# Tying layer-norm statistics to an earlier block's conv1, and moving taps and spectra stores to ScalarE's queue

## The chip, the cores and the metric

The kernel runs on one core of a Trainium2 chip. The metric is the device time of one execution in microseconds. The kernel before was run three times: 1967.88, 1967.87 and 1965.79 us, median 1967.87 us. One more execution was taken with the hardware profiler.

The engines are named as in the profile: PE is TensorE's matmul, PEld its weight load, DVE VectorE, ACT ScalarE, POOL GpSimd and SP SyncE. SPq and ACTq are the places in SP's and ScalarE's instruction streams where DMAs are issued.

## What is computed

Two graph layers run over x of shape 128 graphs × 128 nodes × 256 features, float32. In each layer the input is layer-normalised and rectified, and the layer's output is added to x. The first layer is a convolution branch and a message branch joined by gates like those of a GRU; the second is a sum of five small graph convolutions over fixed subsets of the nodes. What matters here is the convolution branch of the first layer:

```python
h = jnp.maximum(_layernorm(x, axis=-1), 0.0)          # into layer 0
xc = jnp.transpose(x, (0, 2, 1))                      # x is h here
h = _bn(_conv1d(xc, conv1_w, 0), bn1_g, bn1_b, bn1_m, bn1_v)
h = jax.nn.relu(h)
h = _bn(_conv1d(h, conv2_w, 8), bn2_g, bn2_b, bn2_m, bn2_v)
x_conv = jnp.transpose(jax.nn.relu(h + xc), (0, 2, 1))
```

`conv1` is a product with a 256 × 256 matrix. `conv2` has 17 taps along the nodes, and the kernel computes it in a frequency domain.

## The kernel before, in words

A block is four graphs (`BB`, line 18), so there are 32 blocks; a half is 64 graphs (`HG`), or 16 blocks. The kernel has a front part and a gates part. The front part ends at about 530 us, and the change lies in it.

**Weight spectra** (`weight_spectra`, line 153). The taps of conv2 come in eight pieces. For each, `taps_load` (line 147) reads 1024 KB into one of two `w2` buffers, TensorE transforms it in four groups of four PSUM banks (line 160), and the sixteen banks are copied into `sp`, of which there are two buffers: three of each four copies by ScalarE (line 168) and the fourth by VectorE (line 166). The finished `sp`, 2560 KB, is stored to the DRAM tensor `vd` (line 170). SP issues both the loads and the stores.

**Heads** (lines 173 to 272). For block i, `head_load` (line 175) reads 512 KB of x into a buffer `ln`. `head_stats` (line 179) makes mean and variance on VectorE (lines 184, 185, 187) and the power -1/2 on GpSimd (line 189). `head_norm` (line 192) normalises in place on VectorE. `head_turn` (line 198) transposes on TensorE (line 205), rectifies on ScalarE into `ht` (line 206) and stores `ht` to DRAM (line 207). `head_conv1` (line 210) multiplies on TensorE (line 219), adds the shift on VectorE (line 222) and rectifies on ScalarE (line 223) into `h1`. `head_spectra` (line 226) transforms `h1` on TensorE (line 234) into `X`, with copies on VectorE (line 240) and ScalarE (line 242).

The loop in `heads` (line 255) is a software pipeline over i: load block i + `ahead`, conv1 of block i, turn of block i + 1, norm of block i + 2, spectra of block i − 1, statistics of block i + 3. In the first half `ahead` is 5, and twice per block `between()` puts two groups of a weight spectrum in. In the second half `ahead` is 3 and `between()` does nothing.

**Spectral stage** (`spectral`, line 274). For each of 40 frequencies p, the weight spectra `v` are loaded by SP (line 284, two DMAs of 512 KB per pair of frequencies, three `v` buffers). VectorE makes `s` (line 297), GpSimd makes `vs` (line 299, three buffers), TensorE makes three products (lines 302 and 307), ScalarE copies the first to `k1` (line 304) and VectorE adds (line 308); ScalarE issues the stores to `yd` (line 311). Eight frequencies before its end, `near_end` calls `heads_begin` (line 244) for the next half, which loads three blocks of x on SP and starts their statistics.

**Gate weights** (`gate_weights`, line 321). After the first spectral stage in program order stand the loads of `wih` and `whh` (lines 383 and 384) and twelve GpSimd operations (lines 326 to 329), which write the three tiles `sw`. They are used only in the gates part.

**What sets the order.** The program is written as a stream of operations on tiles. A list scheduler orders each engine's instructions by its own estimate of when they are ready, within the dependences between tiles; it therefore may put an operation ahead of others that stand before it in the text. [...] The trace shows such moves: the load of `fw` (line 382) is issued at 36.70 us, amid the first half's heads.

Of the kernel before, what the change touches and what calls it, by code (L numbers as in the profile page):

```python
# [21 lines left out]
NP_ = LW // 2  # L22
WCH = 64
# [51 lines left out]
def gnn_kernel(ctx: ExitStack, tc: tile.TileContext, io, out0: bass.AP, out1: bass.AP):  # L75
    nc = tc.nc
# [15 lines left out]
    def bank():  # L92
        return psum.tile([P, 512], F32, tag="bank", name="bank")
# [50 lines left out]
    vd = dram.tile([C, D // WCH, P, LW, WCH], F32, tag="vd", name="vd")  # L144
    yd = [dram.tile([HG, 2, LW, D], F32, tag=f"yd{h}", name=f"yd{h}") for h in range(NH)]

    def taps_load(pool, c, q, split=1):
        w2 = pool.tile([P, WCH // 4, P], F32, tag="w2", name="w2", bufs=2)
        for t in range(0, WCH // 4, WCH // 4 // split):
            nc.sync.dma_start(w2[:, t:t + WCH // 4 // split], io["w2t"][:, c, q, t:t + WCH // 4 // split])  # L150
        return w2

    def weight_spectra(pool, c, q, w2):

        sp = pool.tile([P, LW, WCH], F32, tag="sp", name="sp", bufs=2)
        for t in range(WCH // 16):
            ps = [bank() for _ in range(4)]
            for j in range(4):
                for r in range(4):
                    nc.tensor.matmul(ps[r][:, j * LW:(j + 1) * LW], w2[32 * r:32 * r + KW, 4 * t + j, :],  # L160
                                     gt[32 * r:32 * r + KW, :], start=True, stop=True)
            for r in range(4):
                o0 = t * 16 + 4 * r
                dst, s = sp[:, :, o0:o0 + 4], ps[r][:, :4 * LW].rearrange("p (j d) -> p d j", j=4)
                if r == 3:
                    nc.vector.tensor_copy(dst, s)
                else:
                    nc.scalar.copy(dst, s)
            yield
        nc.sync.dma_start(vd[c, q], sp)  # L170


    xs, stats, hcs, h1s = {}, {}, {}, {}

    def head_load(pool, ahead, i, queue):
        xs[i] = pool.tile([P, BB, D], F32, tag="ln", name="ln", bufs=ahead)
        queue.dma_start(xs[i], x[i * BB:(i + 1) * BB].rearrange("b n d -> n b d"))

    def head_stats(wk, i):

        mv = wk.tile([P, BB, 2], F32, tag="mv", name="mv", bufs=3)
        st = wk.tile([P, BB, 6], F32, tag="st", name="st", bufs=2)
        for b in range(BB):
            nc.vector.bn_stats(st[:, b, :], xs[i][:, b, :])
            nc.vector.bn_aggr(mv[:, b, :], st[:, b, :])
        ve = wk.tile([P, BB], F32, tag="ve", name="ve", bufs=2)
        nc.vector.tensor_scalar(ve, mv[:, :, 1], EPS, None, op0=ALU.add)  # L187
        rs = wk.tile([P, BB], F32, tag="rs", name="rs", bufs=3)
        nc.gpsimd.tensor_tensor(rs, ve, mhalf, op=ALU.pow)  # L189
        stats[i] = mv, rs  # L190
# [53 lines left out]
    def heads_begin(wk, xk, ahead, h):  # L244

        i = h * NBH
        for k in range(1 if h == 0 else 0, ahead):
            head_load(xk, ahead, i + k, nc.sync)
        for k in range(1 if h == 0 else 0, 3):
            head_stats(wk, i + k)  # L250
            if k < 2:
                head_norm(i + k)
        head_turn(wk, i)

    def heads(wk, xk, ahead, X, h, between):

        i0, i1 = h * NBH, (h + 1) * NBH
        for i in range(i0, i1 + 1):
            if i + ahead < i1:
                head_load(xk, ahead, i + ahead, nc.sync)  # L260
            if i < i1:
                head_conv1(wk, i)
            between()
            if i + 1 < i1:
                head_turn(wk, i + 1)
            if i + 2 < i1:
                head_norm(i + 2)
            between()
            if i > i0:
                head_spectra(X, i - 1)  # L270
            if i + 3 < i1:
                head_stats(wk, i + 3)

    def spectral(bp, X, h, near_end):

        for p0 in range(0, NP_, 4):
            if p0 == NP_ - 8:
                near_end()
            ys = bp.tile([P, 4, 2, D], F32, tag="ys", name="ys", bufs=2)
            for p in range(p0, p0 + 4):  # L280
                if p % 2 == 0:
                    v = bp.tile([P, C, D // WCH, 4, WCH], F32, tag="v", name="v", bufs=3)
                    for c in range(C):
                        nc.sync.dma_start(v[:, c], vd[c, :, :, 2 * p:2 * p + 4, :].rearrange("q i d o -> i q d o"))
                vr, vi = v[:, :, :, 2 * (p % 2), :], v[:, :, :, 2 * (p % 2) + 1, :]
                a, d = X[:, :, p, 0, :], X[:, :, p, 1, :]
                y = ys[:, p - p0]
                ps = bank()
                if p == 0:
                    for k, (u, w) in enumerate(((a, vr), (d, vi))):  # L290
                        for c in range(C):
                            nc.tensor.matmul(ps[:, k * D:(k + 1) * D], u[:, c], w[:, c], start=c == 0, stop=c == C - 1)
                    nc.scalar.copy(y.rearrange("p k o -> p (k o)"), ps)
                    continue

                s = bp.tile([P, C, P], F32, tag="s", name="s", bufs=2)
                nc.vector.scalar_tensor_tensor(s, a, -2.0, d, op0=ALU.mult, op1=ALU.subtract)  # L297
                vs = bp.tile([P, C, D // WCH, WCH], F32, tag="vs", name="vs", bufs=3)
                nc.gpsimd.tensor_tensor(vs, vr, vi, op=ALU.add)  # L299
                p1 = bank()  # L300
                for c in range(C):
                    nc.tensor.matmul(p1[:, :D], a[:, c], vs[:, c], start=c == 0, stop=c == C - 1)  # L302
                k1 = bp.tile([P, D], F32, tag="k1", name="k1", bufs=2)
                nc.scalar.copy(k1, p1[:, :D])  # L304
                for k, (u, w) in enumerate(((s, vi), (d, vr))):
                    for c in range(C):
                        nc.tensor.matmul(ps[:, k * D:(k + 1) * D], u[:, c], w[:, c], start=c == 0, stop=c == C - 1)  # L307
                nc.vector.tensor_tensor(y, ps.rearrange("p (k o) -> p k o", k=2),  # L308
                                        k1[:, None, :].to_broadcast([P, 2, D]), op=ALU.add)
            for w in range(2):  # L310
                nc.scalar.dma_start(yd[h][:, w, 2 * p0:2 * p0 + 8, :].rearrange("g d o -> g (d o)"),
                                    ys[w * HG:(w + 1) * HG].rearrange("p a k o -> p (a k o)"))
# [18 lines left out]
    with front as es:  # L331
# [3 lines left out]
        with ExitStack() as ws:  # L335

            xk = ws.enter_context(tc.tile_pool(name="xk", bufs=1, side="right"))
            wp = ws.enter_context(tc.tile_pool(name="wp", bufs=1))
            ahead = 5
            todo = [(c, q) for c in range(C) for q in range(D // WCH)]  # L340
            head_load(xk, ahead, 0, nc.scalar)
            nc.sync.dma_start(gt, io["gt"])
            taps = [taps_load(wp, *todo[k], split=1 if k else 4) for k in range(2)]
            head_stats(hk, 0)
            head_norm(0)
            spectra = []

            def some_spectra(k=1):
                for _ in range(k):
                    if not spectra and todo:  # L350
                        spectra.append(weight_spectra(wp, *todo.pop(0), taps.pop(0)))
                    if spectra and next(spectra[0], STOP) is STOP:
                        spectra.pop(0)
                        if len(todo) > 1:
                            taps.append(taps_load(wp, *todo[1]))
                        some_spectra()

            some_spectra(3)
            constants()
            heads_begin(hk, xk, ahead, 0)  # L360
            some_spectra(3)
            heads(hk, xk, ahead, X, 0, lambda: some_spectra(2))
            while spectra or todo:
                some_spectra()
        gw = ctx.enter_context(tc.tile_pool(name="gw", bufs=1, side="right", reuse_waits="tile"))
        xk = es.enter_context(tc.tile_pool(name="xk1", bufs=1, reuse_waits="tile"))
# [6 lines left out]
        sw = [gw.tile([P, 3, 3, P], F32, name=f"sw{k}") for k in range(3)]  # L373
# [13 lines left out]
    wk = ctx.enter_context(tc.tile_pool(name="wk", bufs=1, reuse_waits="tile"))  # L387
# [716 lines left out]
```

## Time and profile before

| what | us |
|---|---|
| median of three runs | 1967.87 |
| profiled execution, its own time | 1969.54 |
| profiled execution, span from first to last instruction | 1967.8 |
| TensorE matmul busy | 1911.4 |
| VectorE busy | 1288.8 |
| ScalarE busy | 711.4 |
| GpSimd busy | 610.3 |

The mean granted clock of TensorE is 0.984 of full speed. Busy times of different engines overlap. A row of the profile for a group of instructions gives line, engine, operation, what is written from what is read, the count, the busy time and the mean of one; a bracket after an instruction in order of time gives how long its engine had been idle and what ended that.

The largest transfers of the front part, by the page's list of DMA issues, are:

| transfer | issued by | times | KB each |
|---|---|---|---|
| v from vd | SP | 80 | 512 |
| vd from sp | SP | 8 | 2560 |
| ht to DRAM | ScalarE | 32 | 512 |
| x | SP (one by ScalarE) | 31 + 1 | 512 |
| taps | SP | 7 of 1024, 4 of 256 | |

### The profile page before, as it was taken

The numbers are of one execution on the slowest core, as the hardware profiler recorded it, in microseconds if no ns is written. First come the engines' busy times: TensorE is split into PE (matmuls) and PEld (weight loads), VectorE is DVE, ScalarE is ACT, GpSimd is POOL, SyncE is SP. The second block draws the span as 40 slices with busy tenths as digits, with TensorE's granted clock in tenths as the row PEclk, the third lists the DMA queues.
The fourth block names the chain that finished last, engine by engine and source line by source line (L and its number), as shares of the span: only waits on it lengthen the run. The fifth ranks groups of instructions, "written<-read, shape, count | busy, mean of one in ns | idle before, by whom it ended". The sixth has DMA issues, their size and how long they took to land.

```text
span 1967.8 us, 29919 instructions
## 1 busy us (share of the span) xinstructions
PE 1911.4 (97%) x10418; PEld 1664.8 (85%) x10418; DVE 1288.8 (65%) x3255; ACT 711.4 (36%) x1438; POOL 610.3 (31%) x681
## 2 busy tenths in 40 slices
PE   8889997999999999999999999999999999999998
PEld 7778886998878888888878888888878888888887
DVE  6556445855468777777756677777756677777643
ACT  4444112531133433433434433333434433333334
POOL 1011641115423344344322143343322143343300
PEclk9899998999999999999999999999999999999999
DMA  8885795439863323323423533322423533322135
GB/s 312 324 290 179 229 314 183 164 123 293 282 197 84 90 67 92 89 69 79 121 59 98 129 107 83 95 71 70 123 71 94 130 94 94 84 71 56 51 90 148
DMA packets 248853, 265.76 MB, mean 135 GB/s; under 512 B 106850, under 2 KB 223927, under 8 KB 244223
## 3 DMA queue, kind: packets, MB, share of 16 engines
q1 hardware_dynamic: 240367, 225.58, 39.6%
q10 hardware_dynamic: 8336, 38.28, 5.1%
q8 instruction: 83, 1.36, 0.3%
q14 instruction: 67, 0.55, 0.1%
HBM read 178.66 MB, written 85.14 MB: 134 GB/s over the span
## 4 chain that ended last, share of the span: by engine, by line
PE 89%; DMA 5%; DVE 3%; POOL 1%; issue 1%; ACT 1%; SPq 0%; POOLq 0%; DVEq 0%; ACTq 0%
PE bank L565 44%; PE bank L307 6%; PE bank L471 6%; PE bank L884 5%; PE bank L824 5%; PE bank L219 5%; PE bank L302 3%; PE bank L517 3%; PE bank L453 3%; DMA ln<-in_x_dram 3%; PE bank L234 2%; PE bank L456 1%; PE bank L504 1%; PE bank L803 1%; PE bank L735 1%; PE bank L205 1%
## 5 line engine op out<-in xcount | busy, mean ns | idle before, releaser
L565 PE MATMUL bank<-t,sw 128*128 128x256 f32 x1152 | 290.7, 379 | 0.0
L578 POOL TENSOR_TENSOR u<-u,m 128x256 f32<-128x256 f32 x128 | 93.0, 726 | 595.2 <-ACT m L576 546.3
L565 PEld LDWEIGHTS bank<-t,sw 128*128 128x128 f32 x1152 | 215.6, 190 | 29.7 <-issue 2.3
L565 PE MATMUL bank<-t,wih 128*128 128x256 f32 x768 | 197.2, 379 | 0.0
L565 PEld LDWEIGHTS bank<-t,wih 128*128 128x128 f32 x768 | 143.4, 190 | 19.3 <-DVE u L583 0.5
L219 PE MATMUL bank<-wc,ht 128*128 128x256 f32 x512 | 130.0, 411 | 13.9 <-ACT ht L206 13.2
L299 POOL TENSOR_TENSOR vs<-v 128x512 f32<-128x512 f32 x78 | 101.1, 1315 | 130.1 <-DMA v<-vd 73.7
L219 PEld LDWEIGHTS bank<-wc,ht 128*128 128x128 f32 x512 | 103.7, 207 | 32.1 <-ACT ht L206 16.3
L471 PE MATMUL bank<-wms,ht 128*128 128x259 f32 x512 | 122.3, 381 | 0.0
L884 PE MATMUL bank<-w,hh 128*125 128x256 f32 (+9 forms) x480 | 113.6, 380 | 1.0 <-DVE hh L829 1.0
L565 PE MATMUL bank<-t,whh 128*128 128x256 f32 x384 | 114.4, 379 | 0.0
L565 PE MATMUL bank<-xn,wih 128*128 128x256 f32 x384 | 114.2, 379 | 0.0
L565 PE MATMUL bank<-xc,wih 128*128 128x256 f32 x384 | 114.2, 379 | 0.0
L297 DVE SCALAR_TENSOR_TENSOR s<-X 128x256 f32<-128x256 f32 x78 | 52.5, 675 | 91.9 <-PE bank L307 91.7
L565 PE MATMUL bank<-ht,whh 128*128 128x256 f32 x384 | 110.2, 381 | 0.0
L471 PEld LDWEIGHTS bank<-wms,ht 128*128 128x128 f32 x512 | 97.2, 190 | 14.6
L824 PE MATMUL bank<-ax,w 128*128 128x500 f32 (+8 forms) x416 | 107.0, 396 | 0.2 <-DMA w<-in_w_dram 0.2
L583 DVE TENSOR_TENSOR u<-bank,u 128x256 f32<-128x256 f32 x128 | 53.7, 419 | 74.0 <-PE bank L565 74.0
L189 POOL TENSOR_TENSOR rs<-ve,mhalf 128x4 f32<-128x4 f32 x32 | 32.3, 1009 | 225.2 <-DVE ve L187 225.2
L884 PEld LDWEIGHTS bank<-w,hh 128*125 128x125 f32 (+9 forms) x480 | 84.3, 178 | 19.3 <-DVE hh L829 1.6
L475 ACT ACTIVATE msg<-msg 128x512 f32<-128x512 f32 x64 | 40.3, 630 | 162.6 <-DVE msg L472 160.2
L304 ACT COPY k<-bank 128x256 f32<-128x256 f32 x78 | 28.9, 372 | 178.6 <-DVE ys L308 69.8
(190 smaller groups left out, 4307.1 us busy)
## 6 DMA issues: line engine op xcount, KB each, us to landing
v<-vd SPq DMA_DIRECT2D x80, 512.0 KB
vd<-sp SPq DMA_DIRECT2D x8, 2560.0 KB
yd<-ys ACTq DMA_DIRECT2D x40, 512.0 KB
w<-in_w_dram SPq DMA_DIRECT2D x40, 512.0 KB
htd<-ht ACTq DMA_DIRECT2D x32, 512.0 KB
ht<-htd SPq DMA_DIRECT2D x32, 512.0 KB
ym<-yd SPq DMA_DIRECT2D x32, 512.0 KB
xt<-in_xT_dram SPq DMA_DIRECT2D x32, 512.0 KB
```

Source lines behind the costliest of these rows:

```text
L219: nc.tensor.matmul(pv[:, bb, :], ht[:, c, b * N:(b + 1) * N], wc1[:, c, :], start=c == 0, stop=c == C - 1)
L299: nc.gpsimd.tensor_tensor(vs, vr, vi, op=ALU.add)
L302: nc.tensor.matmul(p1[:, :D], a[:, c], vs[:, c], start=c == 0, stop=c == C - 1)
L307: nc.tensor.matmul(ps[:, k * D:(k + 1) * D], u[:, c], w[:, c], start=c == 0, stop=c == C - 1)
L453: nc.tensor.matmul(ps[:, b * N:(b + 1) * N], ym[:, b, o * P:(o + 1) * P], idm, start=b == 0, stop=False)
L471: nc.tensor.matmul(ps[:, :D + 3], ht[:, c, b * N:(b + 1) * N], wms[:, c, :], start=c == 0, stop=c == C - 1)
L517: nc.tensor.matmul(ps[:, b * N:(b + 1) * N], msg[:, b, c * P:(c + 1) * P], e[:, b, :], start=True, stop=True)
L565: nc.tensor.matmul(ps, w, d, start=n == 0, stop=n == len(pairs) - 1)
L578: nc.gpsimd.tensor_tensor(got["u4"], got["u2"], got["m5"], op=ALU.add)
L583: nc.vector.tensor_tensor(got["u3"], ps, got["u2"], op=ALU.add)
L824: nc.tensor.matmul(pv[:, q - q0, :], w1s[k5 + g][:, c, q * P:(q + 1) * P], xv[:, c], start=c == 0, stop=c == C - 1)
L884: nc.tensor.matmul(ps[:n1, :D], hh[:, q, at:at + n1], w2s[k5 + g][:, q, :], start=q == 0, stop=q == HID // P - 1)
```

## The change

There are four edits. First, `head_stats` takes an optional tile `behind`: if it is given, ScalarE copies one column per graph of it into the statistics buffer `st` before VectorE's statistics overwrite that place. In `heads` the tile is `h1s[i]`, the output of conv1 of block i, for the statistics of block i + 3. Secondly, ScalarE issues the spectra stores and all taps loads but the first two; of the last four copies of a spectrum, the one that VectorE made is made by ScalarE. Thirdly, the first three x loads of the second half are issued by ScalarE in place of SP. Fourthly, at frequency 20 of the first half, GpSimd copies one column of `k1` into each tile `sw`, in a place that the gate weights' first operation writes.

```diff
-    def taps_load(pool, c, q, split=1):
+    def taps_load(pool, c, q, queue, split=1):
         w2 = pool.tile([P, WCH // 4, P], F32, tag="w2", name="w2", bufs=2)
         for t in range(0, WCH // 4, WCH // 4 // split):
-            nc.sync.dma_start(w2[:, t:t + WCH // 4 // split], io["w2t"][:, c, q, t:t + WCH // 4 // split])
+            queue.dma_start(w2[:, t:t + WCH // 4 // split], io["w2t"][:, c, q, t:t + WCH // 4 // split])
...
-                if r == 3:
+                if r == 3 and t < WCH // 16 - 1:
                     nc.vector.tensor_copy(dst, s)
                 else:
                     nc.scalar.copy(dst, s)
             yield
-        nc.sync.dma_start(vd[c, q], sp)
+        nc.scalar.dma_start(vd[c, q], sp)
...
-    def head_stats(wk, i):
+    def head_stats(wk, i, behind=None):
...
+        if behind is not None:
+            nc.scalar.copy(st[:, :, 0], behind[:, :, 0])
         for b in range(BB):
             nc.vector.bn_stats(st[:, b, :], xs[i][:, b, :])
...
-            head_load(xk, ahead, i + k, nc.sync)
+            head_load(xk, ahead, i + k, nc.scalar if h else nc.sync)
...
-                head_stats(wk, i + 3)
+                head_stats(wk, i + 3, h1s[i])
...
+                if h == 0 and p == NP_ // 2:
+
+                    for t in sw:
+                        nc.gpsimd.tensor_copy(t[:, 0, 1, 0:1], k1[:, 0:1])
...
-            taps = [taps_load(wp, *todo[k], split=1 if k else 4) for k in range(2)]
+            taps = [taps_load(wp, *todo[k], nc.sync, split=1 if k else 4) for k in range(2)]
...
-                            taps.append(taps_load(wp, *todo[1]))
+                            taps.append(taps_load(wp, *todo[1], nc.scalar))
```

## The prediction

> **What bounds the kernel now.** I read the page first, then the busy time by stretches of the span, then the waits of TensorE and VectorE inside the stretches that are not full, and last the order of time around the longest waits.
>
> ```profile
> PE 1911.4 (97%) x10418; PEld 1664.8 (85%) x10418; DVE 1288.8 (65%) x3255; ACT 711.4 (36%) x1438; POOL 610.3 (31%) x681
> ...
> PEclk9899998999999999999999999999999999999999
> ```
>
> TensorE is the bound: 1911.4 of 1967.8 us, so idle time can give back at most 56.4 us. A second reserve is the granted clock, which falls below 1 only in the first third of the span. By stretches (length, then busy time of PE, PEld, DVE, ACT and POOL, granted clock, DMA share, GB/s):
>
> ```profile
> 22.20:125.00 102.80, 89.88 (x1106) 78.51 (x1102) 57.30 (x191) 48.98 (x134) 10.06 (x10) 0.87 0.82 305
> 125.00:196.30 71.30, 64.81 (x369) 57.69 (x369) 46.50 (x151) 27.74 (x74) 12.49 (x12) 0.95 0.67 233
> 196.30:215.00 18.70, 15.90 (x67) 13.20 (x66) 7.64 (x11) 2.50 (x7) 16.53 (x16) 0.91 0.51 169
> 295.00:340.00 45.00, 32.83 (x151) 27.36 (x150) 24.03 (x63) 10.45 (x26) 9.31 (x8) 0.85 0.57 181
> 345.00:425.00 80.00, 80.00 (x495) 74.50 (x494) 58.78 (x198) 40.15 (x102) 9.47 (x10) 1.00 0.39 139
> ```
>
> The first row is the heads with the weight spectra, the second the rest of the first half's heads, the third the start of its spectral stage, the fourth the end of that stage and the first heads of the second half, the fifth those heads in full run: TensorE never idle, VectorE idle for 21.2 us. Ceiling of each row, idle plus busy time times (1 − clock): 12.9 + 11.7 = 24.6; 6.5 + 3.2 = 9.7; 2.8 + 1.4 = 4.2; 12.2 + 4.9 = 17.1. Together 55.6 us. The waits between 22 and 125 us (total, times, longest), TensorE's:
>
> ```profile
> PE bank L160 <- DVE sp L166: 10.1, 3, 4.1
> PE bank L234 <- DVE sp L166: 2.1, 4, 0.6
> ```
>
> and one of VectorE's:
>
> ```profile
> DVE st L184 <- DMA ln<-in_x_dram: 9.5, 4, 4.4
> ```
>
> In order of time, one of the two four-microsecond waits:
>
> ```profile
> 47.21 0.33 SPq L170 DMA_DIRECT2D vd<-sp  x1
> ...
> 47.64 0.38 SPq L177 DMA_DIRECT2D ln<-in_x_dram  x1
> ...
> 62.09 0.75 DVE L184 BATCH_NORM_STATS2 st<-ln 128x6 f32<-128x256 f32 x2 [4.31 <-DMA ln<-in_x_dram]
> ...
> 63.76 0.46 DVE L166 COPY sp<-bank 128x320 f32<-128x320 f32 x1
> ...
> 64.28 2.01 PE L160 MATMUL bank<-gt,w 17*128 17x80 f32 x32 [4.02 <-DVE sp L166]
> ```
>
> The load of block 7 is issued 0.43 us after a 2560 KB spectra store on the same queue and is used 14.4 us later. VectorE has already reached that block's statistics, though conv1 has only done blocks 0 to 2 by then; it stands there, and the eviction that TensorE needs stands behind it. The same happens at 105.5 to 109.6 us, and twice in the second half:
>
> ```profile
> 284.38 0.44 SPq L177 DMA_DIRECT2D ln<-in_x_dram  x1
> ...
> 295.34 0.75 DVE L184 BATCH_NORM_STATS2 st<-ln 128x6 f32<-128x256 f32 x2 [6.38 <-DMA ln<-in_x_dram]
> ...
> 297.97 1.48 PE L307 MATMUL bank<-v,s 128*128 128x256 f32 x4 [2.57 <-issue]
> ...
> 315.81 28.95 SPq L177 DMA_DIRECT2D ln<-in_x_dram  x4
> ...
> 324.11 0.75 DVE L184 BATCH_NORM_STATS2 st<-ln 128x6 f32<-128x256 f32 x2 [8.47 <-DMA ln<-in_x_dram]
> ...
> 330.38 6.61 PE L219 MATMUL bank<-wc,ht 128*128 128x256 f32 x16 [6.72 <-ACT ht L206]
> ```
>
> The last row also shows the clock: conv1 of a block takes 6.61 us here and 3.45 us in the chain's undisturbed blocks. At 194.7 us GpSimd starts the twelve gate-weight operations as soon as their load lands, and TensorE's next product waits behind them:
>
> ```profile
> 194.73 1.96 POOL L326 TENSOR_TENSOR sw<-wih 128x384 f32<-128x384 f32 x2 [17.10 <-DMA wih<-in_wih_dram]
> ...
> 208.82 1.14 PE L302 MATMUL bank<-vs,X 128*128 128x256 f32 x4 [2.79 <-POOL vs L299]
> ```
>
> [...] after the 4.02 us wait, 65 to 70 us has a granted clock of 0.51. [...]
>
> **The change, part by part.** The sums are made against the profiled execution, 1969.5 us (span 1967.8), which is 1.7 us above the median of the runs, 1967.9.
>
> *Statistics behind conv1.* Adds 26 ScalarE copies of 128x4 (13 in each half). The nearest row is the 128x5 exponential, 0.23 us: 26 × 0.23 = 6 us of ScalarE, which is busy 49.0 of 102.8 and 40.2 of 80 us, so it hides. VectorE's statistics of block i+3 now wait for the ReLU of conv1 of block i; behind them stand evictions, norms and spectra copies, for which TensorE waits. With x loaded five ahead in the first half, block 7's statistics come after conv1 of block 4, past 84 us, while x was there at 62. The waits at 60 and 105 us go: 4.02 + 4.08 us idle, and the clock with them (65–70: 5.0 × 0.49; 60–65: 0.98 × 0.20; 110–115: 5.0 × 0.42; 105–110: 0.92 × 0.26) = 5.0. Together −13. What is late next is the sp slot: a period moves 2560 + 1024 + 512 + 512 KB = 4.7 MB; the store issues lie 14.7 us apart on average (22.15 to 125.04 in seven periods), 11.4 in the shortest. At the 440 to 455 GB/s of the fullest 5 us stretches the data alone need 10.5 us, and TensorE's work (two times 2.03 for the spectrum, 3.45 + 0.9 + 2.17 for the head) 10.6. A mean of 14.7 − 13/7 = 12.8 us is inside both. Bounds: −5, if stores become late, to −20.
>
> In the second half, block 19's statistics can't stand before conv1 of block 16 at 311 us, so the wait at 295 goes whole: 2.57 + 1.83 idle and about 1.0 of clock = 5.4. For block 20 they follow conv1 of block 17 (ends 320.5), its x lands at 324, and the evictions and the ReLU of block 18's turn are ahead of them: of 1.06 + 6.72 idle and 3 of clock I count half. With 5.4 that is about −10; bounds −5 and −15. In the full run the tie costs nothing while it stays below VectorE's spare 21.2 / 12.3 = 1.7 us per block.
>
> *Taps and spectra stores on ScalarE.* Six tap loads (0.33 us to issue) and eight stores (0.33) leave SP for ScalarE: 14 × 0.33 = 4.6 us. The eight copies that go from VectorE to ScalarE are 8 × 0.44 = 3.5 us there and 3.9 less on VectorE; a store then waits for nothing younger than ScalarE's own copy. SP's waits for them (58.7 for taps, 45.6 for the spectra) leave x's path. A tap load waits for the last product of its spectrum, which ScalarE's next copies need anyway. Behind a store on the ACT row now stand taps and the ht stores; ht is needed again only after 500 us. I take 0 on the path; bounds −3 and +5 if issuing stretches (SP's x loads reached 1.42 us each).
>
> *x of the second half by ScalarE.* Three issues, previously at 145.8 us on SP and 4.3 us long; their statistics and two norms (about 7 us of VectorE) ran amid the heads there, with 6.5 us of TensorE idle. Less crowding on SP and earlier x for blocks 13 to 15: −3, bounds 0 and −7.
>
> *Gate weights held to the middle of the first spectral stage.* Adds three one-column copies on GpSimd, between 0.1 (a memset of 128x4) and 1.0 us (the power) each. It removes the block of 12 operations ahead of L299 at 207 us: −3 of the ceiling 4.2. The twelve (about 1.07 us each, 12.9 in all) then go into a stage in which a frequency takes TensorE 2.6 us and GpSimd 1.3; if they sit in the gaps they cost nothing, in a row 12.9 less three vs buffers (7.8) = 5, plus clock. I take +3.
>
> Sum: −13 − 10 − 3 − 3 + 3 = −26 on the path: 1943.5 for the profiled kind of execution, 1942 against the median.
>
> **Rivals.** *Transfers hold the front.* The 31.5 MB between 22 and 125 us already move at a DMA share of 0.82; stores and taps land later beside x, sp slots come late and the −13 vanishes. For it: the share of 0.8 to 1.1 in most 5 us stretches; against: the 11.4 us period. Then 1968 − 13 = 1955. *All goes*: the tie and the free queue take most of the 55.6: about 1922. *It doesn't do what it says*: the new order has waits of the same size elsewhere, within 3 us of before. *VectorE becomes the bound through the tie (slower).* Per block it is busy 58.78 / 12.3 = 4.8 us of 6.5. If the order puts statistics at once behind conv1's eviction, each block adds the ReLU (0.63), the copy and crossings (0.4), and the wait for GpSimd's power (1.2) before a norm right behind: with the X and conv1 waits that remain (about 0.9), 7.9 us. It decides from 1.7 us of added wait per block; 1.4 us over in each of 23 heads outside the DMA-bound part is 32 us, and clock on top, against some 16 gained: 1984. Against it: one iteration lies between statistics and norm in program order.
>
> **How the numbers follow.** Likeliest, 1942 (its own range 1930 to 1953): 0.52. Transfers hold the front, 1955: 0.22. All goes, 1922: 0.08. No effect: 0.05. VectorE bound, 1984: 0.13. A difference of 0.2%, 4 us, is what a measurement of this kernel can tell. Faster: 0.52 + 0.22 + 0.08 = 0.82; same 0.05; slower 0.13. The range leaves out the slower case and the far half of "all goes": 1926 to 1968.
>
> **What would show it.** VectorE's wait for x in its statistics (34.4 us up to 350) nearly gone; TensorE's L160 waits for sp gone between 50 and 115 us; spectra stores 12 to 13 us apart; no granted clock near 0.5 at 65, 110 and 330 us; the gate-weight operations after 240 us. Wrong: ScalarE waiting for vd stores, or VectorE waiting for ScalarE in statistics with TensorE idle between 345 and 425 us.

## The result and the profile after

The changed kernel took 1970.2 us (median of 4 runs, 1967.4 to 1973.3), the kernel before 1967.9. The ratio is 1.0012, 95% interval 0.9994 to 1.0031: no change that can be measured, where 1942 was forecast, with a range up to 1968. The profiled execution took 1967.4 us, its span is 1965.5.

The page of the changed kernel, busy time by engine and the granted clock in slices of 49 us:

```profile
PE 1910.6 (97%) x10418; PEld 1666.5 (85%) x10418; DVE 1279.2 (65%) x3247; ACT 714.1 (36%) x1472; POOL 610.0 (31%) x684
...
PEclk9788999999999999999999999999999999999999
```

TensorE's busy time is the old one within 1 us. The second, third and fourth slices of the clock have fallen from 8, 9 and 9 to 7, 8 and 8. Lines are numbered anew: conv1 is L222, the add L225, statistics L187, the norm L198, the spectra's product L237 and its copies L243 and L245, the sums of spectra L302, the first products of the spectral stage L295. The same stretches as before, of the changed kernel (length, busy PE, PEld, DVE, ACT, POOL, clock, DMA share, GB/s):

```profile
22.20:125.00 102.80, 90.64 (x992) 78.51 (x993) 43.23 (x138) 46.00 (x129) 7.04 (x7) 0.78 0.74 292
125.00:196.30 71.30, 61.18 (x400) 55.38 (x400) 43.98 (x150) 27.67 (x78) 10.88 (x10) 0.90 0.59 214
196.30:215.00 18.70, 15.36 (x91) 13.76 (x90) 13.67 (x51) 6.73 (x20) 3.37 (x4) 1.00 0.44 156
295.00:340.00 45.00, 43.64 (x225) 38.06 (x224) 22.98 (x52) 12.00 (x30) 16.31 (x13) 1.00 0.88 301
345.00:425.00 80.00, 80.00 (x496) 74.50 (x495) 59.67 (x211) 39.00 (x112) 11.07 (x11) 1.00 0.39 139
```

The fourth row is the gain: idle plus busy time times (1 − clock) was 17.1 us and is 1.4, so 15.7 us came back at the opening of the second half. The first two rows are the loss: 24.6 has become 12.2 + 90.64 × 0.22 = 32.1, and 9.7 has become 10.1 + 6.1 = 16.2. In landmarks: the last spectra store is issued at 134.6 us (before 125.0), the first spectral stage begins at 211.7 (196.3), the second at 426.8 (425.7). What the first half's heads lost, 15.4 us, the stretch between the two beginnings gave back but for 1.1: it took 229.4 us and takes 215.1.

TensorE's waits of the changed kernel between 22 and 125 us (total, times, longest):

```profile
PE bank L160 <- DMA w<-in_w2t_dram: 4.8, 1, 4.8
PE bank L237 <- DVE X L243: 3.7, 5, 0.7
PE bank L237 <- DVE sp L166: 3.3, 4, 1.0
PE bank L222 <- DVE sp L166: 1.4, 1, 1.4
```

The two waits of four microseconds behind statistics (8.1 of the 10.1 us) are gone, as is nearly all of VectorE's waiting for x (4.9 us up to 600 us, before 37.9). Three new things stand there. The first is a wait for taps. In order of time:

```profile
32.91 0.33 ACTq L170 DMA_DIRECT2D vd<-sp  x1
33.91 0.33 ACTq L210 DMA_DIRECT2D htd<-ht  x1
34.27 1.63 ACTq L150 DMA_DIRECT2D w<-in_w2t_dram  x1
...
47.84 3.71 PE L160 MATMUL bank<-gt,w 17*128 17x80 f32 x64 [4.81 <-DMA w<-in_w2t_dram]
```

On ScalarE's row (a DMA queue of its own in the profile, q10: 38.28 MB before, 67.11 after) the taps are issued 1.4 us behind a store of 2560 KB and are used 13.6 us after their issue. Before, SyncE issued them 4.2 us ahead of that store. The second is a small wait for a bank in each block. The third lies at 155 us:

```profile
145.29 0.17 DVE L190 TENSOR_SCALAR ve<-mv 128x4 f32<-128x4 f32 x1
...
154.98 1.26 POOL L302 TENSOR_TENSOR vs<-v 128x512 f32<-128x512 f32 x1 [19.07 <-DMA v<-vd]
156.19 1.02 POOL L192 TENSOR_TENSOR rs<-ve,mhalf 128x4 f32<-128x4 f32 x1
157.25 0.41 DVE L198 TENSOR_SCALAR ln<-ln,mv,rs 128x256 f32<-128x256 f32 x1 [11.79 <-POOL rs L192]
...
159.46 5.04 PE L222 MATMUL bank<-wc,ht 128*128 128x256 f32 x14 [10.08 <-ACT ht L209]
```

GpSimd's fixed list has a sum for the spectral stage ahead of a power of the heads. The sum waits 19.07 us for spectra from DRAM, the power stands behind it (its input was ready at 145.46 us, and it runs at 156.19, right after the sum), VectorE's norm behind the power, and with the norm TensorE's conv1, 10.1 us. In the kernel before, three more powers stood ahead of the first such sum (twelve instead of nine, counted after the power of the constants).

### The profile page after: what moved, and what is told of

Read it like the earlier page. It is cut to its first block, busy times and chain, and to the rows that moved or that the text cites. A ratio compares the mean times of both kernels' runs of the same rounds, so it can differ in the third digit from the quotient of the medians.

```text
span 1965.5 us, 29935 instructions
## 1 busy us (share of the span) xinstructions
PE 1910.6 (97%) x10418; PEld 1666.5 (85%) x10418; DVE 1279.2 (65%) x3247; ACT 714.1 (36%) x1472; POOL 610.0 (31%) x684
## 3 DMA queue, kind: packets, MB, share of 16 engines
q10 hardware_dynamic: 11936, 67.11, 8.5%
## 4 chain that ended last, share of the span: by engine, by line
PE 89%; DMA 4%; DVE 3%; POOL 1%; ACT 1%; issue 1%; SPq 0%; ACTq 0%; POOLq 0%; DVEq 0%
PE bank L572 44%; PE bank L314 7%; PE bank L478 5%; PE bank L222 5%; PE bank L891 5%; PE bank L831 5%; PE bank L305 3%; PE bank L237 3%; PE bank L460 3%; PE bank L524 3%; PE bank L463 1%; PE bank L511 1%; PE bank L810 1%; PE bank L742 1%; PE bank L208 1%; DVE st L187 1%
## 5 line engine op out<-in xcount | busy, mean ns | idle before, releaser
L302 POOL TENSOR_TENSOR vs<-v 128x512 f32<-128x512 f32 x78 | 101.1, 1315 | 141.3 <-DMA v<-vd 99.2
L222 PE MATMUL bank<-wc,ht 128*128 128x256 f32 x512 | 128.7, 408 | 12.8 <-ACT ht L209 11.4
L222 PEld LDWEIGHTS bank<-wc,ht 128*128 128x128 f32 x512 | 104.2, 208 | 29.8 <-ACT ht L209 12.9
L590 DVE TENSOR_TENSOR u<-bank,u 128x256 f32<-128x256 f32 x128 | 53.7, 420 | 73.5 <-PE bank L572 73.5
L237 PE MATMUL bank<-fd,h 128*128 128x160 f32 x512 | 85.3, 323 | 8.4 <-DVE X L243 3.7
```

Source lines behind the costliest of these rows:

```text
L222: nc.tensor.matmul(pv[:, bb, :], ht[:, c, b * N:(b + 1) * N], wc1[:, c, :], start=c == 0, stop=c == C - 1)
L237: nc.tensor.matmul(ps[:, bb * 2 * LW:(bb + 1) * 2 * LW], h1[:, 2 * h + bb, c * P:(c + 1) * P], fd, start=True, stop=True)
```

## The experiments

Changes against the kernel before are given as ratio minus one, times 1967.9 us; a ratio's half interval is about 0.0015, or 3 us, and a difference of two about 4 us. Single executions of one kernel scatter by up to 15 us, and the profiled one may lie at either end.

**The parts on the kernel before.** First the tie alone, that is, the statistics of block i + 3 behind conv1 of block i:

```diff
-                head_stats(wk, i + 3)
+                head_stats(wk, i + 3, h1s[i])
```

> The kernel before with the tie alone (statistics of block i+3 behind conv1 of block i). Theory A (the front's loss comes from ScalarE issuing taps and stores, plus GpSimd's order in front of the first products): the four-microsecond waits of L160 go, spectra stores come at most 14 us apart on average, last store before 122 us; GpSimd still waits for v with a power queued behind it, since the tie moves the powers behind the first vs (TensorE waits 5 to 10 us once between 135 and 160); the waits near 295 and 325 us go (-14). Total 1952 to 1962. Theory B (the tie itself makes the spectra periods longer): stores 16 to 17 us apart, last store after 130 us, total 1966 to 1975. Theory C (transfers bound the front): stores about as before, last store 123 to 127 us, total 1953 to 1960, DMA never idle in a period.

1952.2 us, ratio 0.9935 [0.9910, 0.9959]: −12.8. Next the edit of the issues alone, that is, taps, spectra stores and the last copy:

```diff
-            nc.sync.dma_start(w2[...], ...)
+            queue.dma_start(w2[...], ...)      # nc.scalar, but for the first two
-                if r == 3:
+                if r == 3 and t < WCH // 16 - 1:
-        nc.sync.dma_start(vd[c, q], sp)
+        nc.scalar.dma_start(vd[c, q], sp)
```

> The kernel before with the taps, stores and last copies on ScalarE alone, no tie, x of the second half and gate weights as before. Theory A: taps of the third and fourth piece land late behind a store on ScalarE's row (a wait of L160 for w of about 5 us near 45), periods longer than 14.7 us through ScalarE's issues, last store 130 us or later; no longer GpSimd wait than before; second half's waits at 295 and 325 us still there. Total 1974 to 1984. Theory B: last store at 125 us or earlier and total 1960 to 1969. Theory C: x lands in under 8 us, the waits of VectorE for x in the first half go, stores 14 to 16 us apart, total 1962 to 1972.

2020.4 us, ratio 1.0273 [1.0252, 1.0294]: +53.7. Two lines of its waits between 22 and 200 us, and a stretch in order of time, show why:

```profile
DVE st L187 <- DMA ln<-in_x_dram: 41.1, 8, 12.2
...
PE bank L237 <- DVE sp L166: 24.9, 5, 11.7
```

```profile
39.88 0.37 SPq L177 DMA_DIRECT2D ln<-in_x_dram  x1
39.97 0.33 ACTq L170 DMA_DIRECT2D vd<-sp  x1
40.52 0.33 ACTq L210 DMA_DIRECT2D htd<-ht  x1
40.88 1.37 ACTq L150 DMA_DIRECT2D w<-in_w2t_dram  x1
...
54.38 0.75 DVE L187 BATCH_NORM_STATS2 st<-ln 128x6 f32<-128x256 f32 x2 [11.90 <-DMA ln<-in_x_dram]
```

x is alone on its row and is issued 0.1 us before the store, and still is used 14.5 us later (the next one, again 0.1 us ahead of a store, 14.7). Four later loads are issued 0.7 us ahead of their store and are used after 4.4 to 5.7 us; the first of them:

```profile
97.58 0.37 SPq L177 DMA_DIRECT2D ln<-in_x_dram  x1
98.27 0.33 ACTq L170 DMA_DIRECT2D vd<-sp  x1
...
102.02 0.75 DVE L187 BATCH_NORM_STATS2 st<-ln 128x6 f32<-128x256 f32 x2 [2.69 <-DMA ln<-in_x_dram]
```

In the kernel before, x behind the store on one row was used 14.4 us after its issue. VectorE's list has the statistics right behind the load, ahead of copies that TensorE needs. With the tie the same edit costs far less (below); without it, 53.7 us.

Next the whole change without the edit of the issues (the lines above as they were before), and the whole change without the held gate weights:

```diff
-                if h == 0 and p == NP_ // 2:
-                    for t in sw:
-                        nc.gpsimd.tensor_copy(t[:, 0, 1, 0:1], k1[:, 0:1])
```

> The changed kernel with taps, stores and the last copy as before on SP and VectorE; the tie, x of the second half on ScalarE and the held gate weights stay. Theory A: last store before 122 us, one GpSimd wait of 5 to 10 us for TensorE stays, gate weights cost about 5 us in mid-stage, total 1951 to 1961. Theory B: stores 16 to 17 us apart, total 1966 to 1976. Theory C: between, 1957 to 1967.

> The changed kernel without the three GpSimd copies that hold the gate weights back: the twelve operations run ahead of the first vs again. All theories: the 4.1 us wait of L305 near 280 us goes and one of 2 to 4 us near the start of the stage comes; total within 4 us of the changed kernel, 1966 to 1972.

Without the edit of the issues: 1962.6 us, ratio 0.9983 [0.9973, 0.9993]. Without the held gate weights: 1968.8 us, 1.0007 [0.9998, 1.0017]. The issues cost 5.7 beside the rest. The gate weights are no more than scatter.

**One part of the change undone.** Taps loaded by SyncE, or the stores (and the last copy) as before:

```diff
-                            taps.append(taps_load(wp, *todo[1], nc.scalar))
+                            taps.append(taps_load(wp, *todo[1], nc.sync))
...
-                if r == 3 and t < WCH // 16 - 1:
+                if r == 3:
...
-        nc.scalar.dma_start(vd[c, q], sp)
+        nc.sync.dma_start(vd[c, q], sp)
```

The first edit is one run, the other two together the next.

> The kernel after, with the loads of taps issued by SyncE again; the stores of spectra, the last copies and the x of the second half stay on ScalarE. Without any of the edit of the issues the kernel took 1962.6 us, with all of it 1970.2 us. If the loads of taps carry the cost (each stands behind a store of 2560 KB on its own row, and its 1.3 to 1.6 us of issuing stand ahead of ScalarE's copies of spectra): about 1962.5, the stores fall back from 16.9 to about 16 us apart and the wait of 4.8 us for the taps at 47.8 us is gone. If the stores on ScalarE carry it: about 1970, and the period stays at 16.9 us. SyncE has then taps and x in one list, in the order that the scheduler gives them: an x that waits for a free buffer could hold a tap, which would bring the time above 1970.

> The kernel after, with the stores of spectra issued by SyncE and the last copy of each spectrum on VectorE again; taps stay on ScalarE. If the taps' place behind the store on ScalarE's row is the cost: the store is now on another row, [...] and the time is about 1963. If the taps' issuing ahead of the copies is the cost: about 1969. If the stores themselves were the cost: about 1962, and then the run with the taps put back stays at 1970. SyncE's list then holds a store, which waits for its copies, ahead of the next x: as in the kernel before, x comes late, up to 38 us of waits on VectorE, most of them hidden behind the tie.

Taps back: 1980.5 us, 1.0066 [1.0050, 1.0081]. Above 1970 was expected only if an x held a tap, and the trace shows another cause. In this build VectorE's list has the small maximum over the fusion weights between the two adds of a conv1:

```profile
33.88 0.16 DVE L425 TENSOR_REDUCE fmx<-fw 128x1 f32<-128x5 f32 x1 [7.23 <-DMA fw<-in_fw_dram]
...
34.95 5.15 PE L160 MATMUL bank<-gt,w 17*128 17x80 f32 x56 [5.49 <-DVE h L225]
```

VectorE waits 7.2 us for the 5 numbers, TensorE 5.5, and the clock stays near 0.5 until 49 us. So this run says nothing on taps. Stores back: 1967.2 us, 0.9998 [0.9989, 1.0007], 2.8 below the change, which is within scatter; the wait for taps and the waits for copies of X are gone from its trace.

Whether GpSimd's order costs was tried by tying the first three sums behind the last power of the half:

```diff
         stats[i] = mv, rs
+        powers[i] = rs
...
                 vs = bp.tile([P, C, D // WCH, WCH], F32, tag="vs", name="vs", bufs=3)
+                if h == 0 and p < 4:
+                    nc.gpsimd.tensor_copy(vs[:, 0, 0, 0:1], powers[NBH - 1][:, 0:1])
```

> The kernel after, with the first three sums of spectra that GpSimd makes for the spectral stage tied behind the power of the last block of the first half (three copies of 128x1). In the kernel after, the scheduler put such a sum ahead of a power in GpSimd's list; it waited 19.1 us for spectra from DRAM, and with it the power, the norm, and TensorE's conv1 (10.1 us of wait at 159 us). If that order is the cost: the wait goes, TensorE works on and stage 1 begins 7 to 10 us earlier, about 1961. If the wait only covers another (the last spectra stored late, so that stage 1 waits for its first spectra): stage 1 begins at 211 as before and the time is 1969 to 1971.

1965.4 us, 0.9993 [0.9984, 1.0003]. Stage 1, the first spectral stage, begins at 204.9 instead of 211.7, and the longest wait for ht falls from 10.1 to 4.1 us. In the two profiles the order cost 6.8 us at the start of stage 1; by the ratios it is 3.7 us, which alone would be within scatter, and less than the 7 to 10 expected.

**A base without accidents of order.** The same tie of the sums, on the tie alone:

> The kernel before with the tie, and with the first three sums of spectra on GpSimd tied behind the power of the last block of the first half. The tie alone took 1952.2 us and showed no wait of a norm for a power behind such a sum. If GpSimd's order matters only where it makes a power wait: 1952, within 2. If these sums, now made later, hold the first products of stage 1: 1954 to 1957.

1946.9 us, 0.9898 [0.9882, 0.9914]: −20.1, which is 7 more than expected. The profile of the tie alone was the fastest of its runs (1947.2) and has no such wait, so that part of the difference can't be placed. Stage 1 begins at 196.05 us (before 196.30), stage 2, the second one, at 407.8 (before 425.7): the gain lies between them. This kernel is the base of what follows. On it the parts of the edit of the issues were set one by one, in these four runs with the maximum over the fusion weights tied behind the gate weights:

```diff
+    nc.scalar.copy(fmx, sw[0][:, 0, 0, 0:1])
     nc.vector.reduce_max(fmx, fw, axis=AX.X)
```

> On the kernel of the tie with GpSimd's order fixed (1946.9 us): the loads of taps by ScalarE, and nothing else of the edit of the issues. In this and the next three runs the small sum over the fusion weights is tied behind the gate weights, so that no list of VectorE waits early for that load. If the taps' issuing on ScalarE costs as the stores put back showed (4.6 us): 1951 to 1952. If that difference came from the scheduler's order: within 2 of 1946.9.

> The same base, with the stores of spectra by ScalarE and the last copy of each spectrum on ScalarE; taps on SyncE. By my forecast 0: 1947. If the stores or the last copy stretch the block (a fourth copy of 0.43 us on ScalarE, and taps in SyncE's list ahead of or behind x): 1949 to 1956. If the 1980.5 us of the run with the taps put back came from the stores and not from VectorE's wait of 7.2 us for the fusion weights: 1960 or more.

> The same base, with the last copy of each spectrum on ScalarE only; every load and store on SyncE as in the kernel before. If the copy alone stretches the block: as the run with the stores. If the copy relieves VectorE (which makes TensorE wait 2.0 us in each block for a copy behind two norms): 1940 to 1946. If neither: 1947.

> The same base, with the whole edit of the issues. If its price is that of the runs between (7.6 us with x and gates held in both): 1954 to 1955. If a part of those 7.6 us was GpSimd's order, which differed between them: 1949 to 1952. The wait of 4.8 us for taps behind a store near 47 us, and stores 16.9 us apart, should show again.

| on the base of 0.9898 | us | ratio | against the base |
|---|---|---|---|
| taps by ScalarE | 1950.5 | 0.9906 [0.9891, 0.9921] | +1.6 |
| stores by ScalarE, with the last copy | 1953.5 | 0.9933 [0.9914, 0.9951] | +6.9 |
| last copy by ScalarE alone | 1942.4 | 0.9869 [0.9850, 0.9888] | −5.7 |
| all three | 1959.0 | 0.9944 [0.9925, 0.9963] | +9.1 |

The base itself was not run with the maximum tied. The one pair that differs in nothing else, two kernels with x on ScalarE below, differs by 1.6 us, within scatter. The last kernel shows the wait for taps again (5.2 us at 48 us), and its last stores stand 16.9 us apart. The store itself costs 6.9 + 5.7 = 12.6 us (half interval 5), between two kernels that both have the maximum tied; it hid a gain of the copy that goes with it. Its place in the trace: TensorE's waits between 22 and 125 us, first with copy and store on ScalarE, then with the copy alone:

```profile
PE bank L237 <- DVE sp L166: 4.1, 4, 1.1
PE bank L237 <- DVE X L243: 3.7, 5, 0.7
PE bank L222 <- DVE sp L166: 1.4, 1, 1.4
PE bank L160 <- DVE h L225: 0.7, 1, 0.7
```

```profile
PE bank L237 <- DVE sp L166: 4.8, 5, 1.0
PE bank L222 <- DVE sp L166: 1.0, 1, 1.0
```

With the store on ScalarE, the second half of a block's spectra waits 0.7 us for a copy of the first half; the changed kernel has the same five waits, and the base has none. A block of the first kernel, with times from its first spectrum product:

```profile
81.57 2.50 PE L237 MATMUL bank<-fd,h 128*128 128x160 f32 x8 [1.02 <-DVE sp L166]
...
84.81 2.47 PE L237 MATMUL bank<-fd,h 128*128 128x160 f32 x8 [0.74 <-DVE X L243]
```

and of the second:

```profile
77.03 4.63 PE L237 MATMUL bank<-fd,h 128*128 128x160 f32 x16 [1.02 <-DVE sp L166]
```

5.7 us against 4.6, at granted clocks of 0.59 (81 to 84 us) and 0.50 (84 to 87) in the first and 0.67 (75 to 78) and 0.50 (78 to 81) in the second. Stores are 16.8 us apart with the store on ScalarE (four periods from 61.8 to 129.1 us) and 15.3 with the copy alone (59.2 to 120.3). The third store is issued at 43.7 and 43.6 us, level; over the next five periods, which hold these five waits, the two part by 8.7 us, and stage 1 begins at 198.5 and 187.9. Issuing took 0.33 us in each and delays nothing that the trace shows: ScalarE's ht and its next copies follow at the same distances. What changed is which copy TensorE's next bank waits for. Between 22 and 125 us such waits for copies of X stand in all seven kernels where ScalarE issues the stores, and in none of the other thirteen. That they come from another use of the banks, which the scheduler makes once the store is on another engine, is what this suggests; the trace doesn't number the banks, so it is not shown.

**x of the second half on ScalarE.** On the tie alone; then with GpSimd's order fixed; then also with the fusion weights late:

```diff
-            head_load(xk, ahead, i + k, nc.sync)
+            head_load(xk, ahead, i + k, nc.scalar if h else nc.sync)
```

> The kernel before with the tie, and with the x of the second half's opening issued by ScalarE. The tie alone took 1952.2 us; with the x on ScalarE and the held gate weights beside it 1962.6 us. By my forecast the x on ScalarE gains 3: about 1949. If it is the x that costs (three loads of some 1.3 us of issuing on ScalarE, and a new order of the scheduler's list around them): about 1960. If it is the gate weights: about 1952. If the new order on GpSimd alone decides (a sum of spectra ahead of a power): 1952 plus the wait that TensorE shows near 157 us.

> The tie, the x of the second half's opening on ScalarE, and GpSimd's order fixed as in the run before. Without the fix this took 1958.0 us, with one wait of 10.2 us of TensorE behind the power. If that order was the whole price of the x on ScalarE: 1948 to 1952, and the forecast's gain of up to 3 us for the x shows beside the run before. If issuing three loads on ScalarE costs by itself: 1956 to 1958, and the time is then seen in the stretch from stage 1 to stage 2 or in waits for ht.

> The tie with GpSimd's order fixed and the fusion weights' sum late, and the x of the second half's opening by ScalarE: the run with x on ScalarE before it (ratio 0.9938 against 0.9898 of its base), on the base of the last runs. If the x costs by itself: ratio 0.993 to 0.995 again, and this profile, other than the one before (1950.1 us, which was the fastest of its runs and showed stage 1 at the time of the base), should show a wait between 140 and 215 us. If the 8 us were a matter of the order around the fusion weights or of scatter: 0.988 to 0.991.

1958.0 us, 0.9953 [0.9936, 0.9970]; 1956.0, 0.9938 [0.9923, 0.9953]; 1952.8, 0.9930 [0.9917, 0.9944]. On the base it costs 7.9 and 6.3 us: it is the x, and fixing the order gained only 3. The second of these kernels in order of time:

```profile
149.76 0.34 ACTq L210 DMA_DIRECT2D htd<-ht  x1
150.15 0.88 ACT L245 COPY X<-bank 128x160 f32<-128x160 f32 x4 [4.96 <-DMA v<-vd]
150.88 0.23 ACT L184 COPY st<-h 128x4 f32<-128x4 f32 x1
...
154.54 5.36 PE L222 MATMUL bank<-wc,ht 128*128 128x256 f32 x16 [2.50 <-ACT ht L209]
```

Ahead of this store of ht ScalarE stands 5 us, though ht was finished at 144.7 us. The trace names as what ended the wait a load of v, spectra for the next stage, which neither the store nor the copies behind it need. In the base the same store goes out as soon as ht is done:

```profile
148.42 0.36 ACTq L210 DMA_DIRECT2D htd<-ht  x1
148.82 0.69 ACT L245 COPY X<-bank 128x160 f32<-128x160 f32 x3 [0.24 <-issue]
```

What the store waits for is not shown: in the third kernel ScalarE stands 4.3 us in the same place, put down to a product that had ended 4 us earlier. Behind the store stand the X copies and the tie's copy, so the statistics are late, behind them VectorE's add, the ReLU and the next ht; conv1 waits 2.5 us and takes 5.4 us for its sixteen products (3.6 in the base). In the third kernel the same wait is 2.51 us at 158.6, and the granted clock is 0.79 from 156 to 164 us (1.00 in the base); stage 1 begins at 200.0, 4.0 us behind the base, and stage 2 at 413.6, 5.8 us behind. How much of that is due to this one stall isn't shown.

**The gate weights**, on the kernel with tie, fixed order and x:

> As the run before, with the gate weights held back to the middle of stage 1 as in the change: all of the change but the issues of taps and stores, with GpSimd's order fixed. Unfixed it took 1962.6 us. If the held gate weights pay nothing on balance: within 2 us of the run before. If they cost what the stall in mid-stage shows (4 to 6 us of waits for sums of spectra and a lower clock, less the 3 us at the start of the stage): 2 to 4 us above it. If the order was not the cause: 1962.

1955.5 us, 0.9941 [0.9926, 0.9956]: 0.6 above the run without them, within scatter. Both terms show in the changed kernel: the wait of 2.8 us at the start of stage 1 is gone, and at mid-stage the operations run in a row on GpSimd:

```profile
281.24 1.26 POOL L302 TENSOR_TENSOR vs<-v 128x512 f32<-128x512 f32 x1
...
282.55 2.08 PE L305 MATMUL bank<-vs,X 128*128 128x256 f32 x4 [4.10 <-POOL vs L302]
```

**A version that beats both.** In the base TensorE still waits 12.1 us in six blocks for copies of weight spectra, as two groups in a row, of four banks each, fill all eight (line 90). The first half was written in a finer mix, with one group at a time between halves of a block's spectra:

```diff
                 head_conv1(wk, i)
             between()
+            if h == 0 and i > i0:
+                head_spectra(X, i - 1, (0,))
+            between()
...
             between()
             if i > i0:
-                head_spectra(X, i - 1)
+                head_spectra(X, i - 1, (0, 1) if h else (1,))
+            between()
...
-            heads(hk, xk, ahead, X, 0, lambda: some_spectra(2))
+            heads(hk, xk, ahead, X, 0, some_spectra)
```

> The tie, GpSimd's order fixed, and the first half written in a finer mix: one group of weight spectra between the conv1, the first half of the block's spectra, the turn and the second half, where before two groups came in a row. With two groups in a row TensorE fills all eight banks and waits 2.0 us in each block for copies (12.1 us in six blocks with the tie alone), and runs at half clock for 6 to 9 us of each period of some 16.4 us. If those waits set the period: stores 13 to 14.5 us apart, stage 1 begins 10 to 20 us earlier, 1932 to 1944. If the transfers set it (a share of 0.80 to 0.83 in this stretch): stores stay 15.5 to 16.4 us apart and the time is 1948 to 1953. If the copies only wait elsewhere: no change, or up to 5 us slower.

> The tie, GpSimd's order fixed, the last copy of each spectrum on ScalarE, loads and stores on SyncE, and the finer mix of the first half. The copy gained some 5 us and the mix some 6 on the same base (ratios 0.9869 and 0.9864 of before; the base 0.9898). If they remove different waits: ratio 0.984 or below, 1934 to 1937. If both remove the same wait behind the copies: 0.986 to 0.988, 1941 to 1944. The transfers are the next bound in either case, at a share of 0.82 to 0.83 in this stretch.

The mix on the base: 1941.0 us, 0.9864 [0.9849, 0.9879]. With the last copy on ScalarE too: 1926.9 us, 0.9795 [0.9780, 0.9810], 40 us below the kernel before and more than the two gains added (this kernel has the maximum over the fusion weights tied; in the mix alone TensorE waits 1.2 us behind it, so a part of the surplus may come from there). Its stretch from 22.2 to 125 us, and what is left of TensorE's waits there:

```profile
22.20:125.00 102.80, 100.70 (x1185) 86.52 (x1182) 56.38 (x182) 58.71 (x163) 9.06 (x9) 0.93 0.93 349
```

```profile
PE bank L160 <- DVE sp L166: 1.9, 5, 0.9
```

TensorE is idle for 2.1 us instead of 12.9, the clock is 0.93, and four of the seven periods are 12.2 us long. The DMA share has risen to 0.93 with it; as TensorE itself is busy for 98% of this stretch, these numbers don't tell what bounds it next.

## Why the prediction was wrong, by its steps

*Taps and spectra stores on ScalarE* failed: "I take 0 on the path; bounds −3 and +5". On the clean base they cost 9.1 us, in the change 5.7. I priced the issue (0.33 us) and counted what waits for ScalarE; I put at nothing what a store's move does to the order and the banks of everything else, and the late landing of taps behind a store on its row (used 13.6 us after their issue). Of the parts, the copy gained 5.7, the store cost 12.6, and the taps lie within scatter (+1.6): their wait of about 5 us shows only with a store on the same row. ScalarE waiting for vd stores, my sign for "wrong", hardly came (0 to 1.3 us in the kernels above).

*x of the second half by ScalarE*: −3, bounds 0 and −7, measured +6.3 and +7.9. The sign is wrong. I asked what SyncE gains and not what the move does to ScalarE, which then stood 4.3 to 5.0 us ahead of a store with X copies and the tie's copy behind it.

*Statistics behind conv1, first half* (−13): the waits at 60 and 105 us went, and stage 1 hardly gained from it: the tie alone begins it at 193.3 us, the base at 196.05, the kernel before at 196.3. "A mean of 12.8 us is inside both" compared the period with transfers and with TensorE's work at full clock. It left out the banks: behind two groups in a row TensorE waits 2.0 us for copies, and then runs for some 6 us at half clock (0.50 from 84 to 90 us in the base, where six of the seven periods measure 14.3 to 16.7 us). Transfers, my first rival, were not it: with mix and copy the same bytes went in periods of 12.2 us.

*Statistics, second half* (−10, bounds −5 and −15): right in mechanism and too small; 15.7 us in the changed kernel's stretch, and with the tie alone 17.4 between the beginnings of the two stages. It is nearly the whole gain. So the −20.1 of the tie with a clean order is near the −23 forecast for it by luck: a half that did not come and a half that came out too large. *VectorE becomes the bound* did not come: TensorE is never idle from 345 to 425 us in either kernel.

*Gate weights* (−3 and +3): 0.6, as forecast as far as the scatter of 4 us lets it be told; both terms were seen.

The sum by ratios: tie with a clean order −20.1, issues +9.1, x +7.9, gate weights +0.6 make −2.5; the whole change with GpSimd's order fixed measured −1.4; that order, +3.7, brings it to the change's +2.4. The parts add up within their intervals, which are wider than this agreement. Against the forecast of −26 the largest misses are x (10.9), the issues (9.1) and GpSimd's order (3.7), which the forecast did not have. "It doesn't do what it says", waits of the same size elsewhere, to which I gave 0.05, is what happened. Of my signs, VectorE's wait for x and TensorE's L160 waits for sp between 50 and 115 us went, and the gate-weight operations came after 240 us; but the spectra stores came 16.9 us apart at the end of the stretch instead of 12 to 13, and a clock of 0.50 was granted again from 50 to 60 us.

## What to carry to other kernels

Where a scheduler lays out fixed lists, a moved DMA is two edits: the move, and a new order of every engine; look in the new lists for an instruction that waits for a load and has work of another stage behind it, and pin it by a dependence. Before giving DMAs to an engine that computes, look at what would stand behind them if one had to wait: here ScalarE stood 4.3 to 5.0 us, with copies that TensorE needed behind it. Before counting a period down to its transfers, see whether bursts fill the PSUM banks: mixing copy-heavy groups with products was worth more here than any move of a DMA.

## What the runs showed of the hardware

With the edit of the issues alone, a row of its own gave x nothing where it was issued 0.1 us ahead of a store: 14.5 and 14.7 us, against 14.4 behind it in one row. Between 40 and 56 us the row with x moved 528 packets of 0.52 MB at 11.0% of the engines' time, the row with store, ht and taps 432 packets of 4.19 MB at 63.5%: about as many packets, of a tenth of the size. Issued 0.7 us ahead, x did pass: from 97.6 to 103 us its 528 packets moved beside 44 of the other row (0.90 MB). How two rows share the DMA engines is not shown beyond these two stretches.

In two places waits of 2.0 and 1.02 us were followed by half clock. The base in stretches of 3 us (length, busy PE, PEld, DVE, ACT, POOL, clock, DMA share, GB/s), with one wait of 2.0 us in the second:

```profile
78.00:81.00 3.00, 2.92 (x62) 2.45 (x55) 2.35 (x10) 3.00 (x9) 0.25 (x1) 1.00 0.47 117
81.00:84.00 3.00, 1.02 (x24) 1.02 (x27) 2.18 (x6) 1.19 (x4) 0.76 (x1) 0.89 1.05 437
84.00:87.00 3.00, 3.00 (x23) 2.85 (x20) 0.49 (x1) 1.62 (x5) 0.00 (x0) 0.50 0.99 399
87.00:90.00 3.00, 3.00 (x12) 2.82 (x12) 1.11 (x4) 0.49 (x2) 0.00 (x0) 0.50 1.29 437
```

With the copy on ScalarE, one wait of 1.02 us up to 77.0 us was followed by 0.50 from 78 to 81 us, with TensorE busy throughout. Why the clock fell in these two places is not shown.
